# Attention scores and row maxima from two float32r parts, on half of the array's rows, for two halves of the tokens side by side

## The chip, the cores and the metric

The kernel runs on one core of one Trainium2 chip. Its time is the device time in microseconds from one launch, which covers all 16 batches. Of the kernel before there are three runs: 1107.79, 1110.97 and 1111.06 us, so 1110.97 us in the median. One further execution was recorded by the profiler; it is the source of every row quoted here.

The engines are called as in the profile: PE multiplies matrices (PEld are its weight loads), DVE is the vector engine, ACT the scalar engine, POOL the third elementwise engine, and SP issues the DMAs. Matrix products land in PSUM, which this kernel uses as eight banks of 128 partitions by 512 float32.

## The reference

For each batch (16 of them, T = 512 tokens, C = 256 channels) the input is normalized, and three things are added up: the input, an attention block, and a gated feed-forward block.

```python
q = (xn @ Wq.T + bq) * 16 ** -0.5        # 512 x 256, 16 heads of 16
k, v = split(xn @ Wkv.T + bkv)           # one 16-wide k and v for all heads
p = softmax(q.reshape(16 * 512, 16) @ k.T)   # 8192 x 512 for each batch
out = (p @ v).reshape(16, 512, 16).transpose(1, 0, 2).reshape(512, 256) @ Wo.T + bo
...
return x + out + ffn(xn)                 # 6 experts, top 1, exp and log
```

The attention is the large part: 8192 rows of 512 scores for each batch. The contraction over one head is only 16 long, while the array has 128 rows. The kernel uses the spare rows for precision: q and k are each written as a sum of low-precision parts, the parts are stacked along the contraction, and one matrix product adds up all the cross products.

## The kernel before, in words

**Tiling.** One batch after another, with several in flight. A batch first loads x (`load`), normalizes (`stats` to `norm`), transposes (`trans`) and projects to q (`q`), and to the gate, k and v (`e`). q is split into three bfloat16 parts (`q_split` with `split3`, line 404), and `q_in` (L536) lays seven copies of 16 rows into the tile `qst` with 28 DMAs a batch: 112 rows are q parts (`KR` = 7 * 16). `kv` (L556) makes the matching seven k parts with the order they need, `ks` transposes them, and `ks_ev` copies them into `kst`, whose last 256 columns hold differences of k.

**Row maxima.** `amax` (L700) multiplies for one head and 128 tokens: 112 rows, 512 columns, into one bank of the pool `ps_a` (4 banks, shared with every projection through `bank`). There are 64 of them a batch. `amax_ev` (L705) takes the maximum of each row: ACT applies Relu to half of the bank (L712), and DVE adds the other half and reduces it to one number for each token (L714). That is an operation of 256 columns and then a short read of the accumulator. When the 16 heads of one group `g` are there (four groups a batch), `m_split` (L716) negates and splits them into three bfloat16 parts, `m` transposes these on PE, `m_ev` (L727) copies them out of PSUM, and three DMAs write them as rows 112 to 114 of `qst`.

**Scores and what follows.** `score` (L735) multiplies 115 rows (`KS` = 115: q parts and the negated maximum) by 512 columns (16 heads by 32 tokens) into one bank of the pool `ps_s` (3 banks); 64 a batch. `exp` (L743) is one ACT pass over that bank. `pv` (L749) multiplies four such tiles by v, each into its own 32 output partitions (a quarter of the array's columns), 16 times a batch, into the one bank of `ps_o`. `o_ev` copies that bank out four times a batch, and `den`, `num`, `quot`, `o_split` and `wo` divide by the sums and project. The feed-forward steps (`z`, `s`, `g`, `d`, `fin` and so on) lie between.

**Order.** There is no scheduler at run time: each engine takes its instructions in the order in which the program issues them, and that order is written out by hand. The tables `FIRST`, `SECOND`, `MIDDLE` (batches 2 to 14) and `LAST` give every step of a batch a place; the places of batch b are moved by `PERIOD` * b, all are sorted (L1072), and the steps are issued in that order. Only the order counts, not the unit. The table `OTHER` picks for some steps which engine does them (index 0 is the default of `KINDS`).

**What makes a step wait.** Tiles are reused in turn: a matrix product waits until the engines that read its bank last are done, and PE does not take the next instruction meanwhile. `qst` has three buffers, `jk` one.

Of the kernel before, what the change touches and what calls it, by code (L numbers as in the profile page):

```python
# [22 lines left out]
PERIOD = 16384  # L23
ONCE = {
    "prep_q": -44314,
    "prep_e": -41474,
    "prep_kv": -29182,
    "prep_kv2": -35118,
    "prep_z": -31994,
    "prep_o": -19601,  # L30
    "prep_w": -24961,
    "prep_y": -21806,
    "prep_r": -27315,
    "prep_m": -15646,
    "prep_t": 2346,
    "warm0": -45414,
    "warm1": -52908,
    "warm2": -39217,
    "warm3": -33976,
    "warm4": -43159,  # L40
    "warm5": -62211,
    "warm6": -19885,
    "warm7": -8168,
    "warm8": -5377,
    "warm9": -3241,
}
FIRST = {
    "load": -29954,
    "stats": (-50621, -48821, -68228, -52226),
    "lnexp": -44866,  # L50
    "newton": -44367,
    "norm": (-35760, -38928, -42685, -41599),
    "trans": (-35712, -34431),
    "trans_ev": (-35276, -33086),
    "trans2_ev": (-33301, -32904),
    "q": (-31776, -29588),
    "q_ev": (-31543, -28346),
    "q_split": (-25778, -24300),
    "q_in": (-19000, -15612),
    "e": (-31366, -30180, -30160, -30686),  # L60
    "e_ev": (-30728, -28924, -28433, -26841),
    "kv": -25772,
    "gate": -26667,
    "gate2": -25703,
    "ks": (-17861, -21780),
    "ks_ev": (-15678, -19769),
    "mask": -23946,
    "mask_ev": -23891,
    "z": -24145,
    "z_ev": -21531,  # L70
    "z_split": -19597,
    "s": -18884,
    "s_ev": -18618,
    "s_max": -17789,
    "s_exp": -15560,
    "p_split": -14050,
    "g": -12740,
    "g_ev": -12657,
    "u_split": -11542,
    "resid": (-25426, -16915, -33301, -34181),  # L80
    "d": (-10621, -7260, -11237, -4664),
    "d_ev": (-10110, -6644, -10575, -3692),
    "fin": (-6945, -2758, -5628, 1972),
    "fin2": 2926,
    "amax": (-11052, -13564, -12516, -13439, -11280, -10114, -8697, -11684, -8465, -7529, -9765, -11911, -10021,
        -5486, -5607, -5619, -3663, -2761, -6965, -8650, -5342, -5165, -8915, -4521, -2499, -5134, -2335, -2896,
        -3076, -1610, -1498, -1997, -646, -3573, 92, 2614, 291, -1053, -395, 2607, -213, 1197, 1980, 1727, 2045,
        1288, 921, 1277, 3777, 4271, 3995, 3539, 3432, 3344, 3169, 4032, 3861, 4501, 5117, 3792, 4799, 5772, 6277,
        5876),
    "amax_ev": (-9454, -12616, -11503, -12664, -11159, -9883, -8292, -10979, -7628, -5949, -8729, -11414, -9313,  # L90
        -5294, -5104, -5273, -2983, -2457, -6258, -8281, -5074, -4852, -8572, -3544, -2125, -4691, -1599, -2300,
        -2748, -1379, -1245, -1504, -645, -3369, 394, 3023, 476, -698, 296, 3002, -88, 1938, 2709, 1888, 2749,
        1860, 1112, 1913, 3853, 4334, 4361, 3744, 3644, 3514, 3190, 4332, 3884, 5066, 5705, 3960, 5189, 6018, 6335,
        5899),
    "m_split": (-4260, 126, 3581, 8432),
    "m": (-4223, 1105, 3914, 10201),
    "m_ev": (-4024, 1563, 4105, 10260),
    "score": (-401, -1403, 239, -1920, 742, 1237, 7, 1251, 1068, 417, 1821, 2680, 2496, 2680, 2161, 3451, 3092,
        3651, 4118, 4976, 3620, 4528, 5746, 3812, 7546, 5968, 4964, 5773, 6340, 7742, 5692, 8243, 8810, 7966, 8164,
        6760, 9105, 10187, 9690, 8696, 10531, 9468, 10733, 10072, 11134, 11731, 11624, 10479, 12924, 12285, 13182,  # L100
        13666, 12134, 13775, 14050, 13347, 14519, 15373, 13107, 13838, 15063, 14153, 16092, 15643),
    "exp": (268, -906, 343, -1135, 1111, 2161, 709, 2209, 1158, 774, 2449, 3457, 3077, 2855, 2522, 3661, 3453,
        3879, 4515, 5472, 4205, 5700, 5797, 4088, 8064, 6943, 5578, 6079, 6785, 8216, 5708, 8772, 9691, 8321, 9038,
        7430, 9677, 10406, 9877, 9349, 11407, 10226, 11648, 10634, 11748, 12019, 12181, 10990, 13057, 12880, 13661,
        13778, 13142, 14270, 14986, 13460, 15343, 15566, 13250, 14111, 15418, 15104, 16350, 15731),
    "pv": (1855, 2939, 3914, 4467, 5959, 7002, 8359, 9151, 10147, 10858, 12110, 12603, 14147, 15081, 16188, 16802),
    "o_ev": (5229, 9633, 13155, 16893),
    "den": (16066, 18821),
    "num": (15808, 18519),
    "num2": (24293, 22678),  # L110
    "rec": (20153, 19713),
    "den_out": (23249, 23768),
    "den_in": (24860, 24846),
    "quot": (27494, 25839),
    "o_split": (27494, 26099),
    "wo": (28307, 31926),
    "wo_ev": (28839, 32011),
    "store": 41729,
}
SECOND = {  # L120
    "load": -52297,
    "stats": (-44339, -43080, -47996, -45717),
    "lnexp": -42844,
    "newton": -41490,
    "norm": (-37464, -39184, -38293, -37941),
    "trans": (-35579, -34449),
    "trans_ev": (-34239, -33084),
    "trans2_ev": (-33669, -32258),
    "q": (-31992, -30752),
    "q_ev": (-31362, -29271),  # L130
    "q_split": (-29969, -24587),
    "q_in": (-13031, -7728),
    "e": (-30967, -31462, -29306, -28935),
    "e_ev": (-30685, -30978, -29003, -28132),
    "kv": -24610,
    "gate": -27999,
    "gate2": -24791,
    "ks": (-22501, -24215),
    "ks_ev": (-22324, -23668),
    "mask": -21427,  # L140
    "mask_ev": -20909,
    "z": -21231,
    "z_ev": -20546,
    "z_split": -20526,
    "s": -17703,
    "s_ev": -17485,
    "s_max": -17392,
    "s_exp": -14879,
    "p_split": -12863,
    "g": -11025,  # L150
    "g_ev": -10949,
    "u_split": -10002,
    "resid": (-12707, -16346, -11375, -11884),
    "d": (-7385, -6011, -3361, -3388),
    "d_ev": (-6855, -5773, -3255, -3194),
    "fin": (-2178, -1665, -975, -1376),
    "fin2": 60,
    "amax": (-12053, -8699, -7702, -8484, -9486, -11194, -9616, -8530, -8554, -7678, -9999, -6514, -5486, -7002,
        -6625, -6259, -5928, -3910, -4727, -3126, -5403, -5780, -2076, -247, -5915, -4143, -3204, -2416, -1523,
        -2837, -2534, -1217, -2006, -1061, 1066, 385, 174, 1290, 892, 1339, 2674, 2041, 2669, 2152, 72, 3856, -558,  # L160
        2036, 3388, 2262, 4063, 7006, 3760, 5762, 5499, 3894, 3081, 4326, 3948, 3303, 4532, 7740, 5144, 6230),
    "amax_ev": (-12033, -8175, -7261, -7752, -9441, -10893, -9294, -8152, -7364, -6991, -9539, -6504, -4514, -6304,
        -6228, -6080, -5722, -3459, -4454, -3022, -4668, -5502, -1357, -155, -5556, -3895, -3038, -1524, -1073,
        -2627, -2139, -882, -1039, -821, 1901, 692, 208, 1572, 1059, 1679, 2786, 2204, 2698, 2404, 332, 4277, 380,
        2370, 3562, 2397, 4451, 7263, 3993, 6491, 6177, 4248, 3931, 4508, 4436, 3535, 5119, 8041, 5168, 7060),
    "m_split": (-3160, 177, 4725, 9207),
    "m": (-2836, 1022, 5264, 9207),
    "m_ev": (-2777, 1116, 5517, 9429),
    "score": (-310, 583, 925, 1340, -796, 1036, 419, 518, 3370, 2098, 3025, 1892, 2920, 3491, 4933, 3129, 4085,
        5822, 3522, 6406, 5255, 3985, 4433, 5183, 7519, 6434, 5555, 5521, 6932, 6005, 8192, 8171, 7955, 7771, 8476,  # L170
        9037, 9722, 8916, 7361, 9163, 9962, 12022, 9294, 11674, 9707, 10454, 10888, 10237, 12480, 11663, 12525,
        11395, 13568, 13836, 13275, 12839, 14552, 13062, 13747, 14361, 14423, 14217, 15931, 15619),
    "exp": (-14, 605, 1082, 2144, 217, 1480, 758, 1414, 3944, 2448, 3227, 1926, 3507, 3659, 5073, 3318, 4761, 6420,
        4002, 6700, 5678, 4328, 5304, 5230, 7790, 6832, 5878, 6235, 7254, 7710, 8492, 8407, 8172, 7915, 9035, 9485,
        10096, 9218, 7774, 9692, 10554, 12378, 9750, 12108, 10013, 10995, 11293, 11041, 12648, 12207, 12608, 11966,
        14114, 14133, 13794, 13400, 15210, 13327, 14293, 15816, 15464, 14510, 16706, 15695),
    "pv": (2361, 3828, 4049, 5205, 6834, 7106, 8137, 8980, 9880, 10531, 12580, 13053, 14085, 14801, 16030, 16712),
    "o_ev": (5271, 9530, 13394, 17302),
# [920 lines left out]
```

## Time and profile before

| | |
|---|---|
| median of three runs | 1110.97 us |
| profiled execution: its own time | 1110.16 us |
| profiled execution: span from first to last instruction | 1108.4 us |
| mean granted TensorE clock | 0.976 of full |
| ACT exp, 128x512 (L746), 1024 of them | 587.3 us busy, 618 ns each |
| ACT Relu, 128x256 (L712), 1024 | 366.1 us busy, 395 ns each |
| `amax` products (L703), 1024 | 357.9 us busy, 388 ns each |
| `score` products (L739), 1024 | 356.0 us busy, 384 ns each |
| `pv` records (L754), 2048 | 280.7 us busy, 609 ns each |
| first exp starts | 76.5 us |

How to read it: busy time counts each stretch once even if records overlap. PE's records overlap their successors (a product is still draining while the next one streams), so what a product costs is read from the distance between the starts of two neighbours, not from its record. The same holds, more weakly, for ACT and DVE. From about 200 to 950 us the program is periodic: the pass at L697, which occurs once a batch, starts at 488.64 and 552.39 us, and all starts of that stretch give 63.77 us a batch. All sums below are for one such batch.

### The profile page before, as it was taken

To read this page: it belongs to the slowest core of one execution; us is meant where nothing else is said; L and a number is where in the kernel's file an instruction comes from. 1 tells how busy PE (TensorE), PEld (TensorE's weight loads), DVE (VectorE), ACT (ScalarE), POOL (GpSimd) and SP (SyncE) were. 2 spreads that over 40 slices of the span, in tenths; PEclk is the share of its full clock that TensorE was granted. 3 is DMA by queue.
4 is the path that set the end of the run, shared out by engine and by line. 5 is a ranking of instruction groups with operands and counts; after the bars stand their busy time and mean duration, and the time that the engine had idled before them with its cause. 6 is when DMAs were issued, how large, how long until landed. Compare 5 with 4: busy or idle time off the path is not lost.

```text
span 1108.4 us, 20974 instructions
## 1 busy us (share of the span) xinstructions
PE 1049.8 (95%) x5875; PEld 463.3 (42%) x5877; DVE 880.4 (79%) x3186; ACT 895.0 (81%) x2189; POOL 524.3 (47%) x856
## 2 busy tenths in 40 slices
PE   8788988999999999999999999999999999997998
PEld 5433332444435343444534344443534344342324
DVE  7586876888888888888888888888888888785764
ACT  4256867888888888889888898988888798896995
POOL 5434236554462736446282644537364544723231
PEclk9789998999999999999999999999999999998998
DMA  4201111113121122112112212212221311112111
GB/s 121 53 2 51 38 36 41 36 42 87 46 72 48 60 49 72 44 46 81 40 60 55 74 36 54 75 47 62 53 65 38 82 45 46 46 28 67 36 42 50
DMA packets 103489, 58.83 MB, mean 53 GB/s; under 512 B 24395, under 2 KB 99404, under 8 KB 103372
## 3 DMA queue, kind: packets, MB, share of 16 engines
q1 hardware_dynamic: 103372, 57.49, 19.6%
q8 instruction: 47, 0.77, 0.3%
q14 instruction: 70, 0.57, 0.2%
HBM read 17.89 MB, written 8.90 MB: 24 GB/s over the span
## 4 chain that ended last, share of the span: by engine, by line
PE 70%; DVE 16%; issue 5%; ACT 4%; POOL 3%; DMA 1%; DVEq 0%; SPq 0%; POOLq 0%
PE po L754 19%; PE pA L703 16%; PE ps L739 16%; DVE jk L714 6%; ACT P L746 2%; PE py L387 2%; PE py L389 1%; ACT rl L712 1%; PE py L388 1%; PE pe L387 1%; PE pe L388 1%; PE pe L389 1%; PE pt L507 1%; DVE os L425 1%; DVE w L697 1%
## 5 line engine op out<-in xcount | busy, mean ns | idle before, releaser
L746 ACT ACTIVATE P<-ps 128x512 f32<-128x512 f32 x1024 | 587.3, 618 | 53.2 <-PE ps L739 46.7
L714 DVE CUSTOM_DVE_ANT_0 jk<-pA,rl 128x256 bf16<-128x256 f32 x1024 | 430.0, 420 | 157.0 <-ACT rl L712 73.7
L712 ACT ACTIVATE rl<-pA 128x256 f32<-128x256 f32 x1024 | 366.1, 395 | 76.8 <-PE pA L703 59.3
L703 PE MATMUL pA<-kst,qst 112*128 112x512 bf16 x1024 | 357.9, 388 | 16.3 <-DVE M L714 12.5
L739 PE MATMUL ps<-qst,kst 115*128 115x512 bf16 x1024 | 356.0, 384 | 13.9 <-ACT P L746 12.8
L754 PE MATMUL po<-P,vt 128*32 128x512 f32 x2048 | 280.7, 609 | 2.7 <-DVE os L425 2.0
L739 PEld LDWEIGHTS <-kst 115*128 115x128 bf16 x1024 | 98.3, 98 | 199.4 <-issue 124.0
L703 PEld LDWEIGHTS <-qst 112*128 112x128 bf16 x1024 | 93.2, 99 | 191.1 <-issue 97.3
L754 PEld LDWEIGHTS po<-P,vt 128*32 128x32 f32 x2048 | 43.2, 108 | 107.2 <-issue 82.8
L714 DVE DVE_READ_ACCUMULATOR2_ANT M<- 128x1 f32 x1024 | 84.3, 82 | 0.0
L655 POOL TENSOR_TENSOR fs<-fs,fm 100x512 f32<-100x512 f32 x16 | 20.2, 1263 | 113.9 <-DMA dr<-dc 48.5
L654 POOL PARTITION_ALL_REDUCE fm<-fs x16 | 29.0, 1814 | 95.3 <-DVE M L714 77.5
L398 POOL TENSOR_SCALAR M<-M 128x16 f32<-128x16 f32 x50 | 11.6, 233 | 128.9 <-DVE M L714 112.1
L425 DVE COPY os<-po 128x512 f32<-128x512 f32 x60 | 62.0, 1033 | 0.2 <-PE po L754 0.2
L398 POOL TENSOR_SCALAR xn<-xt,rs,nmr 128x256 f32<-128x256 f32 x58 | 32.2, 564 | 57.6 <-DVE r L490 57.6
L398 POOL TENSOR_SCALAR F<-zu 96x512 fp32r<-96x512 f32 (+1 forms) x31 | 19.9, 642 | 81.9 <-PE pA L703 56.9
L387 PE MATMUL pe<-e1w,X 128*128 128x294 f32 x128 | 49.3, 385 | 6.4 <-ACT e L425 6.4
L387 PE MATMUL py<-wo,O 128*128 128x256 f32 x128 | 41.4, 323 | 1.4 <-POOL O L398 1.3
L402 POOL TENSOR_TENSOR O<-ao,O 128x512 fp32r<-128x512 f32 (+1 forms) x31 | 41.3, 1331 | 2.6
L398 POOL TENSOR_SCALAR qs<-qf 128x512 bf16<-128x512 f32 x64 | 39.9, 624 | 3.6 <-ACT scr_dl L1027 0.7
L402 POOL TENSOR_TENSOR F<-zu,F 96x512 fp32r<-96x512 f32 (+1 forms) x31 | 40.3, 1299 | 2.6
L388 PE MATMUL pe<-e1w,X 128*128 128x294 f32 x128 | 39.2, 306 | 0.0
(215 smaller groups left out, 1551.3 us busy)
## 6 DMA issues: line engine op xcount, KB each, us to landing
qst<-qs SPq DMA_DIRECT2D x448, 64.0 KB
xt<-in_L_attn_x SPq DMA_DIRECT2D x16, 512.0 KB
rb<-dr SPq DMA_DIRECT2D x31, 256.0 KB
out<-y SPq DMA_DIRECT2D x15, 512.0 KB
qst<-mt SPq DMA_DIRECT2D x192, 4.0 KB
dc<-os SPq DMA_DIRECT2D x62, 8.0 KB
dr<-dc SPq DMA_DIRECT2D x62, 8.0 KB
out<-y SPq DMA_DIRECT2D x4, 128.0 KB
```

The lines of the kernel that those rows point to most:

```text
L387: nc.tensor.matmul(ps, a1, b1, start=first, stop=False)
L388: nc.tensor.matmul(ps, a1, b2, start=False, stop=False)
L398: eng.tensor_scalar(dst, src, mul, add, ALU.mult, ALU.add)
L402: engs[1].tensor_tensor(p2, src, p1.bitcast(F32), ALU.subtract)
L425: (eng.copy if eng is nc.scalar else eng.tensor_copy)(dst, src)
L654: nc.gpsimd.partition_all_reduce(fm, self.fs, L, bass_isa.ReduceOp.max)
L703: nc.tensor.matmul(p, self.qst[g // 2][0:KR, h, cols(g % 2)], self.kst[0:KR, HT:], start=True, stop=True)
L712: nc.scalar.activation(rl, p[:, HT:], AF.Relu)
L714: nc.vector.tensor_tensor_reduce(jk, p[:, 0:HT], rl, 1.0, NEG, ALU.add, ALU.max, accum_out=self.M[g][:, h : h + 1])
L739: nc.tensor.matmul(p, self.kst[0:KS, cols(c)], self.qst[g // 2][0:KS, :, cols(hp, 32)], start=True, stop=True)
L746: nc.scalar.activation(self.P_[k // 2][:, k % 2], self.ps.pop(k), AF.Exp)
L754: nc.tensor.matmul(self.po[g][32 * j : 32 * j + 32], lv, self.P_[2 * u + j // 2][:, j % 2], start=c == 0, stop=c == 3)
```

## The change

q and k are split into two float32r parts instead of three bfloat16 parts. Three cross products are kept (`KR` = 48) and the negated maximum has two parts (`KS` = 50), so a product needs at most 50 rows. Two such sets lie in `qst` and `kst`: one from partition 0, one from partition 64. Set u = 0 holds the first 256 tokens of a batch, set u = 1 the other 256. `amax` and `score` now issue two products each, one on rows 0 to 63 and one on rows 64 to 127 of the array, into two banks. Their numbers remain 64 and 64 a batch, of 512 columns each; ACT and DVE process the same number of banks. The groups of 16 heads become two a batch, each with both halves of the tokens: `m_split` is gone, `m` and `m_ev` run twice a batch, and `m_ev` makes the two parts itself (one affine pass, one subtraction) and issues four DMAs. `q_in` runs four times a batch with six DMAs each. All places are new, `OTHER` is new, and some set-up tiles move into tiles that are free at that time.

```diff
-    KR = 7 * D
-    KS = KR + 3
+    KR = 3 * D
+    KS = KR + 2
...
         def q_split(self, j):
-            split3(self.eng("q_split", j), self.qs[:, j], self.qf[j], self.qf[j])
+            qs = self.qs[j] = self.tile(sb2, [128, 2, T], FR, "qs")
+            split(self.eng("q_split", j), qs[:, 0], qs[:, 1], self.qf[j])
...
+        def q_in(self, i):
+            g, j = i // 2, i % 2
+            if g not in self.qst:
+                self.qst[g] = sb3.tile([128, H, 128], FR, tag="qst", name=f"qst{self.b}_{g}")
+            for u in range(2):
+                for r in range(3):
+                    row = 64 * u + r * D
                     nc.sync.dma_start(
-                        self.qst[f][r * D : r * D + D, 8 * j : 8 * j + 8], self.qs[:, j, r % 3, cols(f, HT)]
+                        self.qst[g][row : row + D, 8 * j : 8 * j + 8].bitcast(F32),
+                        self.qs[j][:, r % 2, cols(2 * u + g)].bitcast(F32),
                     )
...
+            kk = self.tile(sb2, [128, 6, 2, D], F32, "kk")
...
+            affine(f, kp[:, :, 0:2], k1.unsqueeze(2).to_broadcast([128, 12, 2, D]))
+            g.tensor_tensor(kp[:, :, 2], k1, kp[:, :, 0].bitcast(F32), ALU.subtract)
...
+                part = kp[:, 2 * (c0 + t) : 2 * (c0 + t) + 2].rearrange("p u a d -> p (u a d)")
+                nc.tensor.transpose(p[:, cols(t)], part.bitcast(F32), ident)
...
         def amax(self, n):
             g, h = n // H, n % H
-            p = self.pA[n] = ps_a.tile([128, T], F32, tag="a", name=f"pA{self.b}_{n}")
-            nc.tensor.matmul(p, self.qst[g // 2][0:KR, h, cols(g % 2)], self.kst[0:KR, HT:], start=True, stop=True)
+            for u in range(2):
+                p = self.pA[2 * n + u] = ps_a.tile([128, T], F32, tag="a", name=f"pA{self.b}_{n}_{u}")
+                rows = slice(64 * u, 64 * u + KR)
+                nc.tensor.matmul(p, self.qst[g][rows, h], self.kst[rows, HT:], start=True, stop=True)
...
         def m_ev(self, g):
+            p = self.pb.pop(("m", g))[: 2 * H, 0:128]
+            mt = self.tile(sb2, [2 * H, 2, 128], FR, "mt")
+            affine(self.eng("m_ev", g), mt[:, 0], p, -1.0)
+            nc.vector.scalar_tensor_tensor(mt[:, 1], p, -1.0, mt[:, 0].bitcast(F32), ALU.mult, ALU.subtract)
+            for u in range(2):
+                for a in range(2):
+                    row = 64 * u + KR + a
+                    nc.sync.dma_start(self.qst[g][row : row + 1].bitcast(F32), mt[u * H : u * H + H, a].bitcast(F32))
...
         def score(self, k):
+            n, c = k // 8, k % 8 // 2
+            hp = 2 * n + k % 2
+            for u in range(2):
+                p = self.ps[2 * k + u] = ps_s.tile([128, T], F32, tag="s", name=f"ps{self.b}_{k}_{u}")
+                rows = slice(64 * u, 64 * u + KS)
+                nc.tensor.matmul(
+                    p, self.kst[rows, cols(c)], self.qst[hp // 4][rows, :, cols(hp % 4, 32)], start=True, stop=True
+                )
...
 OTHER = (
...
-    {"resid2": 1, "m_split2": 1, "num0": 1, "q_ev0": 1, "q_ev1": 2, "s_ev": 2, "m_ev0": 1, "m_ev1": 2, "m_ev2": 1, "m_ev3": 1, "mask_ev": 2},
+    {"trans_ev0": 1, "q_ev0": 2, "q_ev1": 1, "e_ev2": 2, "ks_ev0": 2, "mask_ev": 2, "s_ev": 2, "m_ev0": 2, "m_ev1": 2, "o_ev0": 1},
...
```

In the third entry of `OTHER` (batches 2 to 14), 1 and 2 stand for DVE with `trans_ev`, `q_ev`, `s_ev` and `m_ev`, and for ACT with `e_ev`, `ks_ev`, `mask_ev` and `o_ev`. So one copy each of `e`, `kst` and `os` moves from DVE to ACT, and one of `X` from ACT to DVE. The defaults of the split steps are POOL.

## The prediction

> **What bounds the kernel now.** I read the page's busy shares first (PE 95%, ACT 81%, DVE 79%), then busy time by stretch:
>
> ```profile
> core 0: us, PE busy (x) PEld busy (x) DVE busy (x) ACT busy (x) POOL busy (x), PEclk, DMA share, GB/s
> ...
> 420.00:490.00 70.00, 68.75 (x402) 30.32 (x400) 59.67 (x215) 59.88 (x147) 33.28 (x53) 1.00 0.21 54
> 490.00:560.00 70.00, 68.49 (x397) 30.25 (x390) 59.44 (x216) 60.16 (x148) 37.99 (x60) 1.00 0.21 55
> ```
>
> PE is busy 98% at full clock, but PE records overlap, so I go on to the timeline and take distances between starts:
>
> ```profile
> 529.83 0.40 PE L388 MATMUL pz<-X,zw 128*96 128x512 f32 x1
> 530.06 0.39 PE L389 MATMUL pz<-X,zw 128*96 128x512 f32 x1
> ...
> 571.25 0.38 PE L739 MATMUL ps<-qst,kst 115*128 115x512 bf16 x1
> 571.47 0.38 PE L703 MATMUL pA<-kst,qst 112*128 112x512 bf16 x1
> 571.69 0.38 PE L739 MATMUL ps<-qst,kst 115*128 115x512 bf16 x1
> ...
> 573.83 0.38 PE L739 MATMUL ps<-qst,kst 115*128 115x512 bf16 x1
> 574.14 1.06 PE L754 MATMUL po<-P,vt 128*32 128x512 f32 x8
> 575.13 0.39 PE L387 MATMUL pM<-mw,F 98*128 98x258 f32 x1
> ```
>
> A 512-column product costs 0.22 us in bfloat16 and 0.23 in float32r (`pz`). A `pv` begins 0.31 after the product before it, 0.09 more than 0.22, and takes 1.00. So a batch occupies PE for 128 x 0.218 = 27.9 (`amax`, `score`), 16 x (1.00 + 0.09) = 17.4 (`pv`), and 15.2 for the rest (24 `pe` x 0.135, 24 `py` x 0.116, 12 `pq`, 6 `pz`, 6 `pS` and `pG` x 0.23, 12 `pM` x 0.122, the transposes): 60.5 of the 63.77 us of a batch.
>
> The same timeline of DVE shows a second bound that the busy share hides:
>
> ```profile
> 536.96 0.42 DVE L714 CUSTOM_DVE_ANT_0 jk<-pA,rl 128x256 bf16<-128x256 f32 x1
> 537.31 0.08 DVE L714 DVE_READ_ACCUMULATOR2_ANT M<- 128x1 f32 x1
> 537.57 0.42 DVE L714 CUSTOM_DVE_ANT_0 jk<-pA,rl 128x256 bf16<-128x256 f32 x1 [0.17 <-PE po L754]
> 537.92 0.08 DVE L714 DVE_READ_ACCUMULATOR2_ANT M<- 128x1 f32 x1
> 538.15 0.42 DVE L714 CUSTOM_DVE_ANT_0 jk<-pA,rl 128x256 bf16<-128x256 f32 x1
> 538.50 0.08 DVE L714 DVE_READ_ACCUMULATOR2_ANT M<- 128x1 f32 x1
> 538.50 0.35 DVE L776 RECIPROCAL dc<-dc 128x32 f32<-128x32 f32 x1
> ```
>
> After an accumulator read the next row maximum starts 0.22 later, though the read lasts 0.08 and another kind of operation starts at once (538.50). One maximum after another costs 0.57. In the batch from 500 to 563.8 us the waits that the timeline marks on DVE add up to 3.9 us, so DVE is occupied for about 59.8. ACT packs better: exp to exp 0.476, Relu to Relu 0.263; 64 of each are 47.3, with its other passes about 51. **PE and DVE bound the batch together; ACT has 13 us spare.**
>
> **The change part by part**, for one batch.
>
> *Products in pairs.* 128 products at 0.218 become 64 pairs. A pair costs least one float32r product, 0.23, if both halves stream together; most two in turn, 0.46. No row of the trace uses half the rows. The nearest is `pv`: its four products on four column quarters give eight records, and four start within 0.02 us, eight 0.43-us streams passing in 1.00. That shows side-by-side tiles, with float32 moving, for columns. [...] I take 0.232: 14.9, **13.0 saved**.
>
> [...]
>
> ```profile
> 568.21 0.19 PEld L388 LDWEIGHTS pe<-e1w,X 128*128 128x128 f32 x1
> 568.35 0.19 PEld L389 LDWEIGHTS pe<-e1w,X 128*128 128x128 f32 x1
> ...
> 570.82 0.10 PEld L703 LDWEIGHTS <-qst 112*128 112x128 bf16 x1
> ```
>
> A pair needs two loads. At 0.19 one after the other they would make it 0.38. But these start 0.14 apart, and 0.116 in the `py` series: successive loads overlap. [...]
>
> *Switches.* [...] Laid on one period, the places of `MIDDLE` change between full, half and quarter arrays 59 times, against 32 now. 27 x 0.09 = 2.4, and a first float32r load that nothing hides (0.19 against 0.10) behind each of 16 `pv`: 1.5. Together **+3.9**. PE: 60.5 - 13.0 + 3.9 = **51.4**. That is 87% of a 58.9-us period; where PE was as little busy, between 70 and 210 us (88%), the granted clock was 0.95, and 5% more would bring PE to 54, still below DVE.
>
> *DVE.* Gone in `MIDDLE`: the one `m_split` of four that ran there (556.39 to 558.67: 2.28), one copy of `e` (0.45), of `kst` (0.60), of `os` (0.87). Added: one copy of `X` (0.66). The four `mt` copies become four passes of like size. **-3.5**. The row maxima stay 64, and the new places have 37 of them directly behind another, against 38. DVE: 59.8 - 3.5 = **56.3**.
>
> *ACT.* It gains those three copies (records 0.40, 0.60, 1.05) and loses one of `X` (0.59): +1.5 by records, 1.2 by distances: **52.3**.
>
> *POOL* loses three `m_split` and half of each `q_split`, some 7 us of 33 busy; its rows mostly wait for others, so nothing is booked. *SP*: 24 and 8 DMAs instead of 28 and 12. Ten issues took 6.37 us, so 5 us of queue go, beside other work. One `q_in` of each batch stands only 3500 of 131072 places (1.7 us) behind the last score that reads its buffer; if that score is late, the `dc`, `dr`, `rb`, x and y transfers queued behind wait with it. Its first reader stands 29,000 places, 14 us, later, so I cost this at nothing. The maxima are written 33,000 places, 16 us, ahead of their first score; the last landing takes some 2 us.
>
> *Start.* The first score needs 32 row maxima instead of 16, 16 x 0.57 = 9 us at most; about 30 were placed ahead of it anyway. Between 0 and 9: I take +4. The end's chain is the same.
>
> **Sum.** The greatest occupation falls from 60.5 to 56.3 and moves to DVE. How much is waited on top? If DVE waits as now, 3.9, the period is 60.2; two full engines made each other wait, and PE now has slack, so at best about 1.3 remains, 57.6. Middle: 58.9, that is 4.9 less. Fifteen periods: 73; less 4 at the start: 69. The profiled span 1108.4 becomes 1039; its own execution took 1.8 more, the median 0.8 more than that: **1042 us**.
>
> **Rivals.**
>
> *A, the pair does not run as a pair* (slower). The halves pass in turn, or the two loads do. At 0.46, PE needs 60.5 - 27.9 + 29.4 + 3.9 = 65.9; with its present share (60.5 of 63.77) the period is 69.5, +5.7 x 15 + 4 = 1200. At 0.38 PE needs 60.8 and the period is 64.1: 1120. It decides from about 0.375 a pair on, where PE is back at 60.5. For it: no half-row product in the trace, and 0.19 for a load. Against: `pv` side by side, and loads 0.116 apart.
>
> *B, DVE gets lighter than I count*. POOL's work shrinks, and `DVE L773` takes 0.75 at 543.53 but 1.24 at 561.03 while POOL is busy; waits for `pMt` (0.37 and 0.55 in the batch) halve. With DVE at 54.5 and 1 of waiting: 55.5, 1110.97 - 8.3 x 15 + 4 = 991. Against: the fixed 0.22 stays.
>
> *C, the relief arrives nowhere*. A score pair takes two of three banks, and a row-maximum pair two of four which every projection shares; PE stands at the second product until ACT or DVE frees a bank, and ACT, without work meanwhile, is late for DVE (its Relu ended 73.7 us of DVE's idle time). Period 63.4: 1110. Against: exp takes 0.476, a new bank is filled about 0.4 after it, and two are still full.
>
> **How the numbers follow.** Forecast 57% (its own range 1020 to 1065), B 18%, A 15%, C 10%. A measurement tells 0.3%, 3.3 us, from no change. Faster: forecast, B and a third of C: 78%. Within 0.3%: 4%, all C. Slower: A and a third of C: 18%. The range goes from B's 985 to just above C, 1115; outside are A and a little below B.
>
> **What would show it.** The two `amax` (or `score`) records of a pair start within 0.12 us, and the next pair about 0.23 after the first; over 0.37 I am wrong by A. PE's busy share falls clearly, DVE's and ACT's rise towards 90%. L697 recurs every 58 to 60 us. If PE waits for exp or for the maxima become its main idle time and L697 recurs every 63, it is C. If L697 recurs at 58.9 but the sum misses, the start is wrong: the first exp, at 76.5 now, should come near 80.

## The result, and the profile after

The change makes the kernel **slower: 1176.47 us** in the median of four runs (1173.12 to 1181.95), against 1110.02 us of the kernel before (also four). The ratio is 1.0606, 95% interval 1.0561 to 1.0651. Forecast were 1042 us, range 985 to 1115.

The page of the kernel after, its busy shares and then PE's busy tenths and granted clock in 40 slices:

```profile
PE 1047.7 (89%) x5843; PEld 500.2 (43%) x5845; DVE 853.9 (73%) x3075; ACT 894.1 (76%) x2213; POOL 422.0 (36%) x529
...
PE   7797999989797998979799797979979798998997
...
PEclk9767998989898997989999897998989899898988
```

Every engine has a *smaller* share than before (PE 95, DVE 79, ACT 81 and POOL 47% of a shorter span), and no engine is busy for longer in sum (PE 1049.8 us before, ACT 895.0, DVE 880.4, POOL 524.3): the added time is not added work, something else was waited for. The dips of PE to 7 and of the clock to 8 recur all along. The busy times of the same two stretches as in the prediction:

```profile
420.00:490.00 70.00, 62.87 (x360) 30.03 (x360) 52.11 (x188) 54.53 (x136) 27.30 (x34) 0.90 0.21 48
490.00:560.00 70.00, 62.66 (x363) 30.03 (x361) 52.85 (x191) 55.16 (x138) 27.67 (x35) 0.93 0.19 48
```

In 70 us PE is busy some 6 us less than before, DVE 7 and ACT 5, at a clock of 0.90 to 0.93 instead of 1.00. Cutting the span at the first exp of batches 0, 3, 13 and 15 shows where the 65.6 us went (spans 1108.4 and 1174.0):

| stretch | before | after | difference |
|---|---|---|---|
| to the first exp | 76.5 | 83.3 | +6.8 |
| batches 0 to 2 | 210.3 | 208.5 | -1.8 |
| batches 3 to 12 | 637.0 (63.7 each) | 692.9 (69.3 each) | +55.9 |
| batches 13 and 14 | 127.6 | 128.0 | +0.4 |
| last batch and end | 57.0 | 61.3 | +4.3 |

It is the repeated batch. The timeline of PE after, over one of them, first a place where all goes well and then the place where the batch loses its time:

```profile
571.05 0.50 PE L699 MATMUL pA<-kst,qst 48*128 48x512 f32 x2
571.38 0.40 PE L737 MATMUL ps<-qst,kst 50*128 50x512 f32 x2
571.63 0.58 PE L699 MATMUL pA<-kst,qst 48*128 48x512 f32 x2
...
577.46 0.57 PE L737 MATMUL ps<-qst,kst 50*128 50x512 f32 x2
577.80 0.39 PE L699 MATMUL pA<-kst,qst 48*128 48x512 f32 x1
584.36 1.51 PE L699 MATMUL pA<-kst,qst 48*128 48x512 f32 x3 [6.17 <-DVE M L711]
585.33 0.96 PE L737 MATMUL ps<-qst,kst 50*128 50x512 f32 x2
586.22 1.94 PE L753 MATMUL po<-P,vt 128*32 128x512 f32 x8
```

At 571.05 a pair (x2, two records 3 to 4 ns apart) takes 0.33 to the next pair, and that one 0.25: **the halves do run side by side**. At 577.80 the second product of a pair finds no bank and PE stands for 6.17 us, until a row maximum on DVE (L711; in the kernel before it is L714) frees one. So look at DVE in the same place:

```profile
576.27 0.08 DVE L711 DVE_READ_ACCUMULATOR2_ANT M<- 128x1 f32 x1
576.27 0.35 DVE L777 RECIPROCAL dc<-dc 128x32 f32<-128x32 f32 x1
582.21 1.75 DVE L774 SCALAR_TENSOR_TENSOR ao<-os,mlo,ao 128x512 f32<-128x512 f32 x1 [5.58 <-POOL ao L396]
583.88 0.41 DVE L711 CUSTOM_DVE_ANT_0 jk<-pA,rl 128x256 bf16<-128x256 f32 x1
```

DVE stood too: its next instruction is the second `num2` (L774), the maxima are queued behind it, and it waits for `num`, which POOL makes (L396). POOL:

```profile
571.59 1.81 POOL L648 PARTITION_ALL_REDUCE fm<-fs  x1 [5.95 <-DVE M L711]
580.24 1.25 POOL L649 TENSOR_TENSOR fs<-fs,fm 100x512 f32<-100x512 f32 x1 [6.84 <-issue]
581.49 0.68 POOL L396 TENSOR_SCALAR ao<-os,mhi 128x512 f32<-128x512 f32 x1
```

`num` stands behind `s_max`. The all-reduce (a maximum over partitions, the first part of `s_max`) has a record of 1.81 us, but POOL's next instruction, which reads its result, starts 8.65 us after its start; the profile puts the idle time down to "issue", that is, to nothing that it shows. In all 16 batches the distance is 8.6 to 9.6 us, and 8.5 to 9.7 in the kernel before. In the kernel before, all-reduce, subtraction and `num` lay at 545.40, 554.90 and 557.25 on POOL (9.5 us from the first to the second), and the second `num2` came on DVE only at 561.03, 3.1 us after the end of `num`, without a wait:

```profile
545.40 1.80 POOL L654 PARTITION_ALL_REDUCE fm<-fs  x1 [5.87 <-DVE M L714]
554.90 1.27 POOL L655 TENSOR_TENSOR fs<-fs,fm 100x512 f32<-100x512 f32 x1 [7.69 <-issue]
...
557.25 0.68 POOL L398 TENSOR_SCALAR ao<-os,mhi 128x512 f32<-128x512 f32 x1
...
561.03 1.24 DVE L773 SCALAR_TENSOR_TENSOR ao<-os,mlo,ao 128x512 f32<-128x512 f32 x1
```

In the tables, `MIDDLE` places `s_max` (the all-reduce), `num` and this `num2` 0.05, 0.066 and 0.111 of a period into the batch; before, they stood at 0.018, 0.125 and 0.278. And with the stop comes a bill: the granted clock by stretch (the column behind POOL's busy time).

```profile
574.50:578.50 4.00, 3.69 (x24) 1.61 (x21) 1.98 (x9) 3.92 (x11) 0.00 (x0) 1.00 0.32 76
578.50:581.30 2.80, 0.00 (x0) 0.00 (x0) 0.00 (x0) 0.37 (x2) 1.06 (x1) 1.00 0.18 43
581.30:591.55 10.25, 7.19 (x28) 3.51 (x32) 6.72 (x20) 4.75 (x11) 7.92 (x9) 0.50 0.51 116
```

PE ran at half clock for 10.25 us; the eight `pv` records at 586.22 take 1.94 instead of 1.06. Over the whole run PE had 219 us of half clock, before 56. The waits of the whole run, summed (us in total, times, longest), name the same engines:

```profile
ACT rl L709 <- PE pA L699: 160.9, 109, 7.2
...
PE pA L699 <- DVE M L711: 75.7, 16, 7.1
DVE ao L774 <- POOL ao L396: 71.1, 14, 6.5
```

### The profile page after: what moved, and what is told of

Same layout as the page of the kernel before. It is cut to its first block, busy times and chain, and to the rows that moved or that the text cites. A ratio compares the mean times of both kernels' runs of the same rounds, so it can differ in the third digit from the quotient of the medians.

```text
span 1174.0 us, 20442 instructions
## 1 busy us (share of the span) xinstructions
PE 1047.7 (89%) x5843; PEld 500.2 (43%) x5845; DVE 853.9 (73%) x3075; ACT 894.1 (76%) x2213; POOL 422.0 (36%) x529
## 4 chain that ended last, share of the span: by engine, by line
PE 66%; ACT 14%; issue 8%; DVE 8%; POOL 3%; DMA 0%; DVEq 0%; POOLq 0%; ACTq 0%
PE po L753 18%; PE pA L699 14%; PE ps L737 12%; ACT P L745 8%; ACT rl L709 5%; DVE jk L711 4%; PE pe L385 2%; POOL fs L649 2%; PE py L385 2%; PE pq L385 2%; PE pe L387 1%; PE pe L386 1%; PE pt L500 1%; PE pq L387 1%; PE pq L386 1%
## 5 line engine op out<-in xcount | busy, mean ns | idle before, releaser
L711 DVE CUSTOM_DVE_ANT_0 jk<-pA,rl 128x256 bf16<-128x256 f32 x1024 | 429.9, 420 | 180.0 <-ACT rl L709 103.2
L709 ACT ACTIVATE rl<-pA 128x256 f32<-128x256 f32 x1024 | 382.4, 413 | 168.3 <-PE pA L699 160.9
L699 PE MATMUL pA<-kst,qst 48*128 48x512 f32 x1024 | 307.3, 500 | 80.4 <-DVE M L711 75.7
L737 PE MATMUL ps<-qst,kst 50*128 50x512 f32 x1024 | 283.7, 464 | 15.6 <-ACT P L745 9.4
L699 PEld LDWEIGHTS pA<-kst,qst 48*128 48x128 f32 x1024 | 139.3, 195 | 308.8 <-DVE M L711 218.9
L737 PEld LDWEIGHTS ps<-qst,kst 50*128 50x128 f32 x1024 | 127.6, 195 | 140.1 <-issue 60.0
L774 DVE SCALAR_TENSOR_TENSOR ao<-os,mlo,ao 128x512 f32<-128x512 f32 x31 | 40.8, 1316 | 71.1 <-POOL ao L396 71.1
L711 DVE DVE_READ_ACCUMULATOR2_ANT M<- 128x1 f32 x1024 | 84.2, 82 | 0.0
L396 POOL TENSOR_SCALAR xn<-xt,rs,nmr 128x256 f32<-128x256 f32 x56 | 32.2, 576 | 118.1 <-DVE r L483 118.1
L417 DVE COPY os<-po 128x512 f32<-128x512 f32 (+1 forms) x49 | 50.7, 1035 | 18.0 <-PE po L753 11.9
L385 PE MATMUL pe<-e1w,X 128*128 128x294 f32 x128 | 48.4, 378 | 9.8 <-DVE M L711 9.1
L396 POOL TENSOR_SCALAR F<-zu 96x512 fp32r<-96x512 f32 (+1 forms) x32 | 20.0, 624 | 94.8 <-DVE zu L665 66.6
L687 DVE SCALAR_TENSOR_TENSOR g<-dl,bok 128x256 f32<-128x256 f32 x64 | 48.4, 757 | 0.0
L400 POOL TENSOR_TENSOR qs<-qf,qs 128x512 fp32r<-128x512 f32 x30 | 41.7, 1390 | 2.5
## 6 DMA issues: line engine op xcount, KB each, us to landing
out<-y SPq DMA_DIRECT2D x4, 128.0 KB
```

The lines of the kernel that those rows point to most:

```text
L385: nc.tensor.matmul(ps, a1, b1, start=first, stop=False)
L396: eng.tensor_scalar(dst, src, mul, add, ALU.mult, ALU.add)
L400: engs[1].tensor_tensor(p2, src, p1.bitcast(F32), ALU.subtract)
L417: (eng.copy if eng is nc.scalar else eng.tensor_copy)(dst, src)
L687: nc.vector.scalar_tensor_tensor(self.g1[:, t], self.dl[:, t], EXP_ZERO, bok, ALU.is_lt, ALU.add)
L699: nc.tensor.matmul(p, self.qst[g][rows, h], self.kst[rows, HT:], start=True, stop=True)
```

## Experiments

Theory: the loss is the wait of `num2` on POOL, with the half clock behind it. Rivals: pairs on half of the rows are themselves slow (loads, changes between the full and the half array, banks), or the period is set by DVE or by ACT. Each number is to be compared with some 1110 us of the kernel before, measured beside it.

**e1: `num` on DVE.** Nothing is left of the wait for POOL.

```diff
-    {..., "m_ev0": 2, "m_ev1": 2, "o_ev0": 1},
+    {..., "m_ev0": 2, "m_ev1": 2, "o_ev0": 1, "num1": 1},
```

> The changed kernel, with num of the second half on DVE instead of POOL for batches 2 to 14 (one entry in the table of engines); no place is moved. Theory 1 (one wait: num2 on DVE stands behind num on POOL, which stands behind the partition maximum; PE is then starved 6.2 us a batch and its clock halved for 10.2 us): num2 no longer waits, L691 recurs every 59 to 61 us instead of 69.3, clock above 0.96, time 1035 to 1065. Theory 2 (the pairs of half-array products, with a load exposed at each change of array mode, bind PE; the wait is only a symptom of slack): the period stays above 66 and the time above 1140.

Measured: 1112.51 us (1107.32 to 1117.57), ratio 1.0035 (1.0010 to 1.0059): the time falls as theory 1 says, but stops far above its 1035 to 1065 us. The span falls from 1174.0 to 1115.8, and of these 58.2 us batches 3 to 12 give 57.2 (692.9 to 635.7). No idle time of PE in them is longer than 0.9 us. The busy times of the same stretches in e1:

```profile
420.00:490.00 70.00, 67.36 (x396) 33.21 (x393) 57.36 (x211) 60.35 (x152) 28.66 (x34) 0.98 0.21 51
490.00:560.00 70.00, 67.59 (x407) 33.00 (x406) 57.78 (x213) 61.28 (x154) 30.79 (x37) 1.00 0.24 57
```

So one place in an order cost nearly all of the loss. But what is left is no gain: the kernel with it repaired is 0.35% above the one before, and PE is busy 96% again though its 128 products now run as 64 pairs. A batch at full clock does take less, 62.3 us against 63.7. Batches 3 to 12 have 27 us of half clock, though (before 3.4), and so take 63.6 in the mean; the first exp comes 8.1 us later than before, and the last batch and the end take 7.3 us more.

**e2, e3: the same wait, taken away by order.** `num` stays on POOL, the second `num2` comes later on DVE: fully, and half-way.

```diff
-    "num2": (115587, 145645),
+    "num2": (115587, 162000),
```

(e3: 154000.)

> The changed kernel with only the place of the second num2 of batches 2 to 14 moved later, from 145645 to 162000, so that DVE takes other work first; num stays on POOL behind the partition maximum. Theory 1: as in the run with num on DVE, period 59 to 61 us and 1035 to 1065 us, since only DVE's order matters. Theory 2: above 1140. A third theory, that POOL itself became late and the whole feed-forward chain with it, would keep the period above 66 here but not in the run that takes num off POOL.

> The changed kernel with the second num2 of batches 2 to 14 moved only by a few instructions (place 154000), some 2.5 us of other DVE work, so that about 3.3 of the 6 us of its wait remain. If the lost time is the idle time alone: PE idles some 3.5 us a batch, the period falls by about 2.7 to 66.6, time about 1140. If half of the loss is the halved clock after the idle time, and a shorter idle time keeps the clock: period 63 or less, time about 1090, clock above 0.95.

Measured: e2 1125.63 us, ratio 1.0151 (1.0129 to 1.0172); e3 1150.07, ratio 1.0359 (1.0323 to 1.0394). In e3 PE is still idle for 4.0 to 6.0 us at one place of each batch, with a stretch of halved clock behind it. DVE's wait for `num` adds up to 71.1 us in the changed kernel, 40.7 in e3 and 5.9 in e2, and batches 3 to 12 take 69.3, 67.0 and 64.8 us each: the loss goes with the length of the wait. How it divides between the wait and the half clock behind it is not separated, since e3 has both. e2 stays 13 us above e1; it has more half clock in these batches (41 us against 27), and why is not shown.

**e4: the wait put into the kernel before.**

```diff
-    "num2": (16645, 20940),
+    "num2": (16645, 18500),
```

> The kernel before with only the place of the second num2 of batches 2 to 14 moved earlier, from 20940 to 18500, so that it is next to its num, which POOL does behind the partition maximum there too. Theory 1: DVE waits about 6 us a batch, PE idles about as long, the clock halves, the period grows from 63.8 by 8 to 10, time 1210 to 1240. Theory 2: the kernel before has the bfloat16 products and takes the wait up: below 1130.

Measured: 1182.62 us, ratio 1.0672 (1.0644 to 1.0700), less than theory 1 expected and far above theory 2. Batches 3 to 12 take 70.4 us each instead of 63.7, and the waits of DVE have a new row, the second one here, with a longest wait like that of the changed kernel (6.5):

```profile
DVE jk L714 <- ACT rl L712: 76.5, 140, 7.0
DVE ao L773 <- POOL ao L398: 56.1, 11, 6.6
```

With no product on half of the rows, an early `num2` makes a loss of the same size (it stands even closer behind its `num` than in the changed kernel). With e1 that settles nearly all of the 66 us. The other experiments ask where the forecast's gain went, and all but e10 start from e1.

**e5: no halves side by side.** Both products of a pair use rows 0 to 63, which is to make them follow each other; the second half's maxima and scores are then computed from the first half's tokens.

```diff
-                rows = slice(64 * u, 64 * u + KR)
+                rows = slice(0, KR)
...
-                rows = slice(64 * u, 64 * u + KS)
+                rows = slice(0, KS)
```

> The run with num on DVE (1112 us), with both products of every pair on rows 0 to 63 of the array, so that they can only follow each other; the row maxima and scores of the second half of the tokens are then computed from the first half's. It measures what side by side is worth in this order. If the half-array pairs deliver their 0.24 us and PE is what binds (theory P): 64 pairs x 0.2 more, period 63 + 10 to 14, time 1260 to 1330. If PE mostly waits inside the pairs for banks that ACT and DVE free (theory W, a ring of waits): the serial pairs fill waits, period 63 + 0 to 5, time 1115 to 1190.

Measured: 1364.19 us, the median of only two runs, 1348 and 1380. Much of that is half clock (485 us in the profiled execution of 1380, mean clock 0.825), which reaches even above the range of theory P, so I compare batches at full clock: 70.1 us against 62.3 in e1. Side by side is worth some 8 us a batch; it is real.

**e6, e10: a lighter PE.** The third product of each float32r projection is left out (`pe`, `pq`, `py` and the rest), in e1 (e6) and in the kernel before (e10).

```diff
-        nc.tensor.matmul(ps, a1, b2, start=False, stop=False)
-        nc.tensor.matmul(ps, a2, b1, start=False, stop=last)
+        nc.tensor.matmul(ps, a1, b2, start=False, stop=last)
```

> The run with num on DVE, without the third of the three products in each float32r projection (the small correction is left out of q, e, z, s, g, d and wo): about 30 products and 4.5 to 5 us of PE less a batch, everything else equal. Theory P (PE binds the steady state at 63): period 58.5 to 60, time 1045 to 1070. Theory W (DVE and the ring of waits through banks bind): period 62 or more, time above 1095.

> The kernel before without the third of the three products in each float32r projection, the same cut as in the run with less PE work: 4.5 to 5 us of PE less a batch. If DVE (59.8 us in the prediction's count) bounds with PE: period 61 to 63, time 1070 to 1095, full clock as before. If PE alone bounds the kernel before: period 59 to 60, time 1045 to 1060. If it is a lower PE load as such that halves the clock, half-speed stretches appear here too; if it is the half-array products, none do.

Measured: e6 1081.78 us, ratio 0.9720 (0.9676 to 0.9763); e10 1088.32, ratio 0.9801 (0.9785 to 0.9818). Some 4 to 4.5 us of products are gone in each batch, and the period falls by 1.4 in both (62.3 to 60.9 at full clock, 63.7 to 62.3). e6 lies between its two forecasts; e10 is where it was expected if DVE bounds the kernel before together with PE. PE still counts, but only a third of what it is relieved of arrives.

**e7, e8: a lighter DVE, a lighter ACT.** e7: the row maximum covers 128 of the 256 columns on DVE. e8: in addition Relu covers 128 columns on ACT.

```diff
-                jk, p[:, 0:HT], rl, 1.0, NEG, ...
+                jk[:, 0:128], p[:, 0:128], rl[:, 0:128], 1.0, NEG, ...
...
-            nc.scalar.activation(rl, p[:, HT:], AF.Relu)
+            nc.scalar.activation(rl[:, 0:128], p[:, HT : HT + 128], AF.Relu)
```

> The run with num on DVE, with DVE's row maximum over 128 instead of 256 columns (half of the keys' pairs are left out of the maximum): about 64 x 0.13 = 8 us of DVE less a batch, same order, same waits for Relu. Theory W: period 58 to 60, time 1040 to 1070, since DVE frees the banks of the maxima sooner. Theory P: period 62 or more, time above 1095.

> The run with num on DVE, with Relu and the row maximum over 128 of 256 columns each (half of the keys' pairs are left out of the maximum): ACT 64 x 0.11 = 7 us and DVE 8 us less a batch. The DVE half alone changed nothing. If the second product of a score pair waits in PE's queue for a bank that ACT frees late (theory W, ring through ACT): PE's waits inside pairs shrink, period 59 to 61, time 1050 to 1080. If the products themselves with their exposed loads and switches fill PE (theory P): period 62 or more, above 1095.

Measured: e7 1110.02 us, ratio 0.9993 (0.9964 to 1.0022); e8 1104.63, ratio 0.9934 (0.9896 to 0.9971). In e7 DVE is busy 48.3 instead of 57.4 us in the stretch from 420 to 490, and an undisturbed batch still takes 62.5 (e1: 62.2 to 62.5):

```profile
420.00:490.00 70.00, 66.63 (x401) 32.21 (x400) 48.34 (x205) 58.81 (x149) 29.24 (x35) 0.98 0.23 56
```

**DVE's busy time does not set the period** of e1. In e8 the period is 64.8 in the profiled execution (1113 us, the slowest of the six), with 6.8 us of halved clock in every batch, so it can't tell what ACT is worth at full clock.

**e9: neighbouring pairs woven.** Where, in the order of PE, a pair of `amax` and one of `score` follow each other, the first half of one goes with the other half of the other, so that each of the two waits for a bank of another pool.

```diff
-            for u in range(2):
+            for u in halves:
...
+            for v in halves:
+                u = 1 - v
...
-    for place, jobs, name, args in sorted(order, key=lambda job: job[0]):
+    for jobs, name, args in woven([job[1:] for job in sorted(order, key=lambda job: job[0])]):
```

> The run with num on DVE, with products of row maxima and scores that are neighbours in PE's order woven: first half of the one, other half of the other, then the remaining two. Two neighbours still use different halves of the array, but each such pair needs one bank of each pool instead of two of one. If what was missing is that second products wait for a bank (about 5 us a batch by the trace): period 59 to 61 and time 1050 to 1085. If exposed loads and switches are all of it: unchanged, 1105 to 1120.

Measured: 1115.44 us, ratio 1.0028 (0.9998 to 1.0057). More pairs start both products together (75% against 61% in e1), but PE is occupied by them as long as in e1, 26 us a batch. Nothing is gained.

**e11, e12, e13: the short waits before the stretches of halved clock.** e1 still has five such stretches between 400 and 950 us (24 us in all), the kernel before one. Ahead of most of them lies a short wait of PE for POOL's second part of O:

```profile
503.81 0.39 PE L387 MATMUL py<-wo,O 128*128 128x256 f32 x1 [0.87 <-POOL O L400]
```

e11 puts `wo` and its copy later, e12 does so in e9, e13 puts a step of `fin` behind the copy of `pG` in e11.

```diff
-    "wo": (172370, 177498),
-    "wo_ev": (177181, 179746),
+    "wo": (176900, 181200),
+    "wo_ev": (181700, 184000),
...
-    "fin": (9839, 45098, 37590, 22570),
+    "fin": (9839, 45098, 39500, 22570),
```

(The last two lines are e13's alone.)

> As e1, with the output projection's matmuls placed 4,530 and 3,700 units later (of 131,072, about 2 us), so that they come after POOL's split of O. If the stretches of halved clock in e1 come from TensorE's own 0.9-us wait for that split, the wait and most of the stretches go, the period is 62 to 62.5 us in every batch and the time 1095 to 1105 us, faster than the kernel before by 0.5 to 1.2%. If they come with the short half-array products as such, they stay and the time stays at 1108 to 1116 us.

> As e9 (neighbouring products of maxima and scores woven), with the same later place of the output projection. By the first theory 1093 to 1105 us, within 0.3% of e11 since weaving did nothing to the occupied time in e9; by the second 1108 to 1120 us. If weaving does pay once the disturbed stretches are gone, this run is below e11 by 5 us or more.

> As e11, with one elementwise step of the feed-forward block (the third of four that follow d) placed behind the multiplication that frees the bank of pG, which in e11 stood behind it on DVE and held up TensorE for 1.0 to 1.3 us a batch. If such waits make the stretches of halved clock, those between 400 and 950 us go (three in e11), the period is 62.2 in each batch and the time 1100 to 1110 us. If the stretches come by themselves, three or more remain there and the time stays at 1114 to 1121 us.

Measured: 1117.84, 1117.30 and 1120.57 us; ratios 1.0083 (1.0061 to 1.0104), 1.0077 (1.0053 to 1.0101) and 1.0077 (1.0049 to 1.0104). In e11 the 0.87-us wait is gone, but PE waits 0.7 to 1.3 us a batch for `zu` on DVE instead; in e13 that one is gone too, and waits of 0.3 to 0.4 us remain. Stretches of halved clock between 400 and 950 us: 3 in e11, 4 in e12, 5 in e13, each in one trace. The first theory falls in all three: taking the longest wait away does not take the stretches away, and it gives no time.

**e14: the two parts in bfloat16.** e13 with the stacked parts of q, k and the maximum as bfloat16 instead of float32r (the kernel before has three parts in this format): the same products, rows and places. With the format change the weight load (0.19 us in e13, 0.10 in e14), the distance between pairs that follow one another (0.241 and 0.220) and the bytes of the DMAs of q and the maximum (half, by the types of the tiles).

```diff
-            qs = self.qs[j] = self.tile(sb2, [128, 2, T], FR, "qs")
+            qs = self.qs[j] = self.tile(sb2, [128, 2, T], BF, "qs")
...
-                self.qst[g] = sb3.tile([128, H, 128], FR, tag="qst", name=f"qst{self.b}_{g}")
+                self.qst[g] = sb3.tile([128, H, 128], BF, tag="qst", name=f"qst{self.b}_{g}")
...
-            mt = self.tile(sb2, [2 * H, 2, 128], FR, "mt")
+            mt = self.tile(sb2, [2 * H, 2, 128], BF, "mt")
...
-    kst = [const.tile([128, T + HT], FR, name=f"kst{i}") for i in range(NK)]
+    kst = [const.tile([128, T + HT], BF, name=f"kst{i}") for i in range(NK)]
```

> As e13, with the two parts of q, k and the maximum as bfloat16 instead of float32r (less exact; the products, their rows, places and number are the same). If float32r loads cost what I worked out, 0.10 us at each of about 28 entries into a run of pairs, the products of maxima and scores occupy TensorE for about 23 us a batch instead of 26, and of that 1 to 2.5 us reach the period: 1070 to 1095 us. If the pair is long because its second product waits for a bank, not for its load, the occupied time stays above 25 and the time within 8 us of e13.

Measured: **1082.10 us**, ratio 0.9749 (0.9722 to 0.9775), faster than both kernels. It has as many stretches of halved clock as e13 (five, 20 us, between 400 and 950), so their number is not the difference. The timeline of e13, products and then loads (PEld), at a place where a run of pairs begins:

```profile
500.78 0.40 PE L387 MATMUL pG<-F,gw 100*98 100x512 f32 x1
501.10 0.50 PE L699 MATMUL pA<-kst,qst 48*128 48x512 f32 x2
501.44 0.40 PE L737 MATMUL ps<-qst,kst 50*128 50x512 f32 x2
...
501.10 0.19 PEld L699 LDWEIGHTS pA<-kst,qst 48*128 48x128 f32 x2 [0.40 <-issue]
501.21 0.19 PEld L737 LDWEIGHTS ps<-qst,kst 50*128 50x128 f32 x2
```

and of e14:

```profile
500.41 0.40 PE L387 MATMUL pq<-X,wq 128*128 128x512 f32 x1
500.74 0.39 PE L699 MATMUL pA<-kst,qst 48*128 48x512 bf16 x2
500.96 0.38 PE L737 MATMUL ps<-qst,kst 50*128 50x512 bf16 x2
501.27 1.06 PE L753 MATMUL po<-P,vt 128*32 128x512 f32 x8
...
500.73 0.10 PEld L699 LDWEIGHTS <-qst 48*128 48x128 bf16 x2 [0.37 <-issue]
500.75 0.10 PEld L737 LDWEIGHTS <-kst 50*128 50x128 bf16 x2
```

In both, the first pair starts 0.32 to 0.33 after a full-array product. In float32r the next pair starts 0.34 after it, in bfloat16 0.22. Over 250 to 950 us the medians of this first distance are 0.337 (some 190 cases) and 0.226 (177), those of later ones 0.241 and 0.220 (33 cases in each run: most runs of pairs are only two pairs long). There are 310 entries into a run of pairs in that stretch of e13, 28 a batch: 28 x 0.11 = 3.1 us. `amax` and `score` together occupy PE for 26.2 us a batch in e13 and 23.3 in e14, 2.9 less, and the period of batches 3 to 12 goes from 63.5 to 61.85. The whole span loses 41.1 us: 2.5 to the first exp, 7.8 in batches 0 to 2, 16.5 in batches 3 to 12, 6.4 in batches 13 and 14, and 7.9 in the last batch and the end, which e14 brings back to 58.8 (before: 57.0). e14 also moves half the bytes of q by DMA, which no run separates; DVE's row maximum takes 420 ns in both.

## Why the prediction was wrong

**The step that failed: POOL.** "*POOL* loses three `m_split` and half of each `q_split`, some 7 us of 33 busy; its rows mostly wait for others, so nothing is booked." I counted POOL's work and not its order. I compared places around `q_in` and the maxima, but did not lay the new place of `num2` against `s_max` and `num`, which it needs, though the trace of before shows that POOL, once the all-reduce has started at 545.40, starts nothing more for 9.5 us. Of the 65.6 us, e1 returns 58.2. The rows of before would have given the price: there `num` ends 12.5 us after the start of the all-reduce, while the new tables put `num2` only 0.06 of a period, 3.9 us, behind it, which gives an estimate of 8 to 9 us of wait a batch. The run shows 5.5 to 6.5 us in most batches, 71.1 in sum.

**"How much is waited on top?"** I took 1.3 to 3.9 us because DVE and PE now left each other slack. Stalls of DVE of nearly 6 us were not in that range, nor was the half clock that came with them (10.25 us at 0.50 in the batch shown). I had "5% more would bring PE to 54" for a clock of 0.95; after shows 0.90 to 0.93 in the same stretches.

**Products in pairs: the mechanism held, the size did not.** A pair alone costs 0.24 (e13, behind another pair), and the halves run together. The forecast's 0.232 was twice the 0.116 between two loads of the `py` series, an estimate; that halves run side by side no row of before showed. Rival A falls: e5 shows that two in turn would cost 8 us a batch. But 14.9 for 64 pairs, with 3.9 of switches, was 18.8, and e13 measures 26.2 (before: 28.6, where I had 27.9). So 2.4 us come off PE where 9.1 were counted, and of the 4.9 us by which the period was to fall, a batch of e1 at full clock shows 1.4. From e13's distances: 64 x 0.241 = 15.4; at 28 entries 0.096 more for the first load, 2.7; at 28 exits 0.09 for the change back to the full array, 2.5. That is 20.6. This 0.09 I had from one place, the start of `pv` 0.31 after a product instead of 0.22; that a change between the full and the half array costs as much was an estimate, which no run showed then. The trace of after shows it: `pz` starts 0.34 after a pair (557.00 to 557.34) and `py` 0.33 (598.12 to 598.45), against 0.24 from a later pair to the next (592.68 to 592.92), and a pair starts 0.32 after `pz` (558.56 to 558.88), against 0.23 from `pz` to `pz`. The other 5.6 is time inside runs of pairs, and it goes with waits for a bank: only 58% of the pairs start both products together. Of the products inside runs that start over 0.36 us after the one before them (105 between 250 and 950 us), 103 start within 0.1 us of the end of an instruction that they wait for: for `ps` an exp on ACT (39), for `pA` mostly an operation on DVE that reads another product out of the shared banks (`e`, `dl`, `zu` or `X`, 48), and a row maximum only 7 times. These 103 add up to some 3 us a batch beyond the 0.24 of a pair. That is what rival C named, and it fits e7, which made only the row maximum lighter. It was not shown by removing it: weaving (e9) did not shorten it, and more banks were not tried. That e1 comes to 1112 us and C had 1110 is in part luck: C's period of 63.4 is not the 62.3 at full clock, and half clock, start and end make up the rest.

**The load that I booked too seldom.** A load lasts 0.19 us in float32r (e13) and 0.10 in bfloat16 (e14), and no run shows more of the cause than that. I took the 0.116 between loads, and for loads behind other pairs that was right (0.241 between pairs). I booked what stays exposed only behind the 16 `pv`, 1.5 us; it is there at each of the 28 entries. In e14, where the load takes 0.10 instead of 0.19, the extra at an entry is gone (0.226 against 0.337), as expected of this term. The 1.65 us a batch and the 41 us of span that e14 gains are what the format is worth as a whole, with shorter distances between later pairs (0.220 against 0.241) and half the bytes; the load is the largest part of it that the distances show.

**DVE as the new bound** fell with e7: 9 us less of DVE in 70 us change nothing. Rival B, which gained by a lighter DVE, falls with it. PE's occupation did not fall to 51.4 but to about 61 (26.2, `pv` 16.0, the rest 18.7). I had 15.2 for the rest, but counted by the same distances it was 17.9 in the kernel before already, and PE there was occupied for 62.5, not 60.5: the sum started too low. So PE remained first, but no engine alone gives the period: PE relieved by 4 to 4.5 gives 1.4 (e6, e10).

**Start and end.** The first exp was to come near 80; it comes at 83.3 (e1: 84.6). "The end's chain is the same": the last batch and end take 4.3 us more in after, 7.3 in e1. Against e13, e14 gets back 2.5 at the start and 7.9 at the end. Half clock was not in this part of the sum: in the last batch and the end it lasts 6 us before, 17 in after and 24 in e1, and up to the first exp 26, 31 and 37. What else makes the start late is open.

What stays open: what starts the short stretches of halved clock, what ACT is worth at full clock, and what more banks would give.

## What to carry to other kernels

When an order is rewritten by hand, take each engine's list and ask for every moved step what it needs and what that stands behind on *its* engine (here the maxima stood behind one `num2` for 5.58 us, and its `num` behind an all-reduce); busy time does not tell it, since a record (1.81 us here) can be far shorter than the time until the engine's next instruction starts (8.65). When matrix products move to part of the rows, count the entries into runs of them (28 for 64 pairs here), and price at each the load that nothing hides and the change between the part and the whole of the array (0.10 and 0.09 us here). And two products that need two banks at once should be laid against every reader of these banks, the copies of other steps too; in this case the trace points to that, and no run removed it.

## What the hardware showed that I had not expected

- After an all-reduce over partitions on POOL with a record of 1.81 us, the next instruction of POOL started only 8.65 us (before: 9.5 us) after its start. That instruction reads the result; whether another could start sooner was not tried.
- In the changed kernel PE had no product running from 578.19 to 584.36 us, and its granted clock was 0.50 from 581.30 to 591.55, for 10.25 us. It halved after far less idle time, too: in e11 stretches of 3.4 us began at 505.1 and 692.9 us when PE had been without a running product for 1.26 and 1.02 us of the 3.4 before, in e13 for 0.65 us at two places. Nor does such idle time decide it: in e1 the 3.4 us up to 631.4 us had 1.21 without a product, and the clock stayed full.
